# Graph layers on one core: the first range as eight plain products, row sums from sums of quarters, norm steps on ScalarE

## The chip, the core and the metric

One core of one Trainium2 chip runs the whole program. The metric is device time in microseconds (us) of one execution. A ratio in this text is the mean time of one kernel's fast runs over the mean of the fast runs of the kernel before in the same rounds on the same chip, so it is not quite the ratio of the medians that are quoted beside it; its interval is 95%.

Engines: PE is TensorE, PEld its weight loads, DVE is VectorE, ACT is ScalarE, POOL is GpSimd, SP is the engine that issues most loads (SPq its queue). L288 is line 288 of the kernel in question; line numbers differ between kernels.

## The reference, cut to what matters

The program has four layers of a graph network on 2708 nodes with 512 features; `adj` is 2708 x 2708, dense in memory. The change touches layer 0 ("sweep 0" in this text) and, for row sums, layer 1's attention ("sweep 2").

```python
mask = adj > 0                                            # layer 0
head = mask / sqrt(sum(mask, -1))                         # one number per row: a count
inc  = adj + head
x = layernorm(x + (inc @ x) / sum(inc, -1))               # product, row sums, norm
# ... layer 1: e = where(adj != 0, exp(-leaky(scores)), 0)
#              x_a = (e @ h) / (sum(e, 1) + 1e-5)         # row sums again
# ... layers 2 and 3: four more products with adj
```

So a range of output rows can be multiplied only after the rows' nonzero entries have been counted, and divided only after the rows of `inc` have been summed.

## The kernel before

Each product with the adjacency is cut into four *ranges* of 256 to 384 columns (r = 0 to 3). In a range the adjacency (transposed) falls into quarters 11, 12, 21, 22 and X into B11, B12, B21, B22; one level of a Strassen-like scheme replaces eight products of quarters by seven, P1 to P7, at the price of sums on VectorE. A product is 22 f32 matmuls. `at(position, f)` puts work at a position counted in products, and from these positions the order of every engine's queue is fixed when the kernel is built (not by position alone, as the traces below show): at run time each engine works through its own queue and waits: in the changed kernel a preparation of VectorE whose row was ready at 45.3 us began at 50.12, behind seven operations of its queue that waited for their load until 47.55.

```python
FIRST = dict(P1=0, P2=1, P7=2, P5=3, P6=4, P4=5, P3=6)    # order of products in range 0
RING = 44                                                 # one ring of [128, 384] buffers

def count_tile(R0, n, h, i, t=None):      # count the nonzeros of output half h
    if t is None:
        t = trans("cl")                                   # a slot of the same ring
        nc.sync.dma_start(out=t[:w, :n], in_=adjT[...])   # loaded for the count alone
    m = mask_tile()                                       # 3 buffers
    nc.scalar.activation(m[:w, :n], t[:w, :n], AF.Sign)
    nc.scalar.activation(m[:w, :n], m[:w, :n], AF.Relu)
    ...
        nc.tensor.matmul(cnt[h][...], m[...], ones_bf[:w, 0:1], ...)

# extra0, range r: the counts of the NEXT range lie among this range's products
for h, p in ((0, 1.0), (1, 3.8)):
    for i in range(NT):                                   # NT = 22 tiles
        at(pb + p + 2.5 * i / NT, lambda i=i, h=h: count_tile(R1, n1, h, i))
    at(pb + p + 2.55, lambda h=h: count_row(R1, n1, h))

def prep0(r, R0, n, h, hj, k, a):         # adj + head, then the running row sum
    t = trans("s")
    nc.vector.scalar_tensor_tensor(t, a, 0.0, row[R0, h], ALU.is_gt, ALU.mult)
    nc.vector.tensor_tensor(a, a, t, ALU.add)
    add_run(R0, h, n, w, a)                               # 44 additions a range

def layernorm(dsts, y, w):
    ...
    nc.gpsimd.tensor_tensor(rstd[:w, 1:2], rstd[:w, 0:1], neg_half[:w], ALU.pow)
    for d, c0, c1 in dsts:
        nc.vector.tensor_scalar(d[:w], y[:w, c0:c1], mv[:w, 0:1], rstd[:w, 1:2],
                                ALU.subtract, ALU.mult)
```

## Time and profile before

Median 3285.5 us (3284.5 to 3289.4). Columns: stretch, its length, then busy us and instructions of PE, PEld, DVE, ACT, POOL, then granted TensorE clock, DMA share, GB/s. Kernel before, ranges 0 to 3 of sweep 0:

```profile
61.06:151.40 90.34, 83.71 (x480) 68.78 (x480) 64.59 (x197) 43.51 (x98) 4.59 (x6) 0.96 0.55 165
151.40:283.47 132.07, 124.17 (x527) 74.27 (x527) 104.00 (x264) 47.82 (x101) 12.07 (x19) 0.93 0.64 162
283.47:423.01 139.54, 125.67 (x555) 76.24 (x554) 105.22 (x273) 45.62 (x102) 17.76 (x29) 0.95 0.60 132
423.01:533.96 110.95, 103.63 (x442) 73.24 (x441) 95.69 (x275) 6.12 (x12) 28.48 (x51) 0.95 0.68 140
```

| | before |
|---|---|
| first product starts | 61.1 us |
| range 0, then ranges 1 + 2 + 3 | 90.3, then 382.6 us |
| sweep 1 starts, and from there to the end | 534.0, 2754.3 us |

### The profile page before, as it was taken

The numbers are of one execution on the slowest core, as the hardware profiler recorded it, in microseconds if no ns is written. First come the engines' busy times: TensorE is split into PE (matmuls) and PEld (weight loads), VectorE is DVE, ScalarE is ACT, GpSimd is POOL, SyncE is SP. The second block draws the span as 40 slices with busy tenths as digits, with TensorE's granted clock in tenths as the row PEclk, the third lists the DMA queues.
The fourth block names the chain that finished last, engine by engine and source line by source line (L and its number), as shares of the span: only waits on it lengthen the run. The fifth ranks groups of instructions, "written<-read, shape, count | busy, mean of one in ns | idle before, by whom it ended". The sixth has DMA issues, their size and how long they took to land.

```text
span 3288.3 us, 35613 instructions
## 1 busy us (share of the span) xinstructions
PE 3166.4 (96%) x12046; PEld 2050.3 (62%) x12046; DVE 1648.1 (50%) x4093; ACT 567.6 (17%) x1126; POOL 349.1 (11%) x604
## 2 busy tenths in 40 slices
PE   3998999999999999999999999999999999999998
PEld 2755566556765555764556865568656587655675
DVE  6687687334346865975223333323244243643444
ACT  4432500000025544641000000000000000000000
POOL 2001023000000010113000010000011011300000
PEclk9999998999999999999999999999999999999999
DMA  6665665422434342553432453324444344533340
GB/s 201 205 145 121 169 97 138 93 70 50 93 81 111 100 134 80 147 163 118 108 98 72 121 159 90 108 71 116 130 128 125 89 142 130 179 112 99 108 128 33
DMA packets 268683, 383.21 MB, mean 117 GB/s; under 512 B 35199, under 2 KB 230071, under 8 KB 268500
## 3 DMA queue, kind: packets, MB, share of 16 engines
q1 hardware_dynamic: 231096, 291.61, 34.0%
q0 software_dynamic: 28688, 78.49, 7.6%
q10 hardware_dynamic: 8716, 10.84, 1.1%
q8 instruction: 95, 1.56, 0.2%
q14 instruction: 88, 0.72, 0.1%
HBM read 325.31 MB, written 55.49 MB: 116 GB/s over the span
## 4 chain that ended last, share of the span: by engine, by line
PE 83%; issue 6%; DVE 4%; DMA 4%; POOL 2%; ACT 0%; SPq 0%; POOLq 0%; ACTq 0%; DVEq 0%
PE accu L283 21%; PE accc L283 20%; PE accd L283 20%; PE acca L283 10%; PE ps_d L381 8%; DMA cl<-in_adjT 1%; PE ps_n L367 1%; POOL B L177 1%; POOL rstd L343 1%; DMA a<-in_adjT 1%; PE ps_t L373 1%; PE pz L606 1%; DVE T L158 0%; DVE run L444 0%; DVE s L449 0%
## 5 line engine op out<-in xcount | busy, mean ns | idle before, releaser
L250 DVE TENSOR_TENSOR a<-a,a 128x384 f32<-128x384 f32 (+4 forms) x988 | 485.0, 507 | 260.1 <-DMA a<-in_adjT 107.8
L283 PE MATMUL accu<-a,B 128*128 128x384 f32 (+5 forms) x1232 | 395.1, 464 | 0.0
L283 PE MATMUL accc<-s,T 128*128 128x384 f32 (+5 forms) x1232 | 373.3, 458 | 3.6 <-DVE s L250 3.6
L283 PE MATMUL accd<-a,B 128*128 128x384 f32 (+5 forms) x1232 | 376.4, 451 | 0.0
L283 PE MATMUL acca<-a,B 128*128 128x384 f32 (+5 forms) x1232 | 367.7, 452 | 0.0
L283 PE MATMUL accd<-a,T 128*128 128x384 f32 (+5 forms) x1232 | 364.2, 453 | 0.3 <-DVE a L250 0.3
L283 PE MATMUL accu<-a,T 128*128 128x384 f32 (+5 forms) x1232 | 360.6, 450 | 0.0
L283 PE MATMUL accc<-a,T 128*128 128x384 f32 (+5 forms) x1200 | 354.5, 452 | 0.0
L250 DVE TENSOR_TENSOR s<-a,a 128x384 f32<-128x384 f32 (+4 forms) x332 | 166.8, 506 | 318.2 <-PE accc L283 263.7
L283 PEld LDWEIGHTS accc<-s,T 128*128 128x128 f32 (+1 forms) x1232 | 233.8, 194 | 115.8 <-issue 6.7
L283 PEld LDWEIGHTS accd<-a,T 128*128 128x128 f32 (+1 forms) x1232 | 233.3, 191 | 114.6 <-issue 2.4
L283 PEld LDWEIGHTS accu<-a,B 128*128 128x128 f32 (+1 forms) x1232 | 233.0, 196 | 111.5 <-issue 23.8
L283 PEld LDWEIGHTS accu<-a,T 128*128 128x128 f32 (+1 forms) x1232 | 231.7, 190 | 110.5
L283 PEld LDWEIGHTS accc<-a,T 128*128 128x128 f32 (+1 forms) x1200 | 226.1, 190 | 112.6 <-ACT W L304 2.2
L283 PEld LDWEIGHTS accd<-a,B 128*128 128x128 f32 (+1 forms) x1232 | 226.5, 190 | 106.2 <-issue 13.5
L283 PEld LDWEIGHTS acca<-a,B 128*128 128x128 f32 (+1 forms) x1232 | 228.6, 190 | 102.9
L311 DVE TENSOR_TENSOR W<-W,accd 128x384 f32<-128x384 f32 (+2 forms) x56 | 28.1, 505 | 313.9 <-PE accd L283 311.7
L311 DVE TENSOR_TENSOR W<-W,U 128x384 f32<-128x384 f32 (+2 forms) x56 | 28.3, 509 | 280.2 <-ACT U L304 279.2
L444 DVE TENSOR_TENSOR run<-run,a 128x384 f32<-128x384 f32 (+5 forms) x328 | 165.2, 505 | 0.6
L343 POOL TENSOR_TENSOR rstd<-rstd,neg_half 128x1 f32<-128x1 f32 (+1 forms) x88 | 54.8, 623 | 1039.8 <-DVE rstd L342 1034.0
L304 ACT COPY U<-accu 128x384 f32<-128x384 f32 (+2 forms) x56 | 24.4, 439 | 584.9 <-PE accu L283 583.7
L641 ACT ACTIVATE e<-row,neg_s 128x384 f32<-128x384 f32 (+4 forms) x176 | 100.8, 573 | 96.5 <-DVE a L644 32.1
(178 smaller groups left out, 2997.6 us busy)
## 6 DMA issues: line engine op xcount, KB each, us to landing
a<-in_adjT SPq DMA_DIRECT2D x560, 192.0 KB
a<-in_adjT SPq DMA_DIRECT2D x280, 165.0 KB
a<-in_adjT SPq DMA_DIRECT2D x273, 128.0 KB
cl<-in_adjT SPq DMA_DIRECT2D x80, 192.0 KB
ld<-X SPq DMA_DIRECT2D x60, 256.0 KB
Y<-y POOLq DMA_DIRECT2D x54, 256.0 KB, 2.3
B<-Y POOLq DMA_DIRECT2D x84, 128.0 KB, 3.4
X<-o POOLq DMA_DIRECT2D x36, 256.0 KB, 3.2
```

What stands on the lines that cost most here:

```text
L177: eng.dma_start(out=t[:w], in_=q)
L250: nc.vector.tensor_tensor(A[r, dst, k][:w, :n], A[r, a, k][:w, :n], A[r, b, k][:w, :n], op)
L283: nc.tensor.matmul(B[home, c][:, :n], X[STAT[p], k][:w, c * P : (c + 1) * P], A[r, MOV[p], k][:w, :n], start=bool(start and k == k0), stop ...
L304: nc.scalar.copy(T[nm, c][:, :n], B[home, c][:, :n])
L311: nc.vector.tensor_tensor(d[:, :n], T[t, c][:, :n], o[:, :n], ALU.add)
L343: nc.gpsimd.tensor_tensor(rstd[:w, 1:2], rstd[:w, 0:1], neg_half[:w], ALU.pow)
L367: nc.tensor.transpose(ps[:w, c * P : (c + 1) * P], C[h, c][:, lo : lo + w], ident)
L373: nc.tensor.transpose(ps[:, c, :w], cols(dsts, c)[:w], ident[:w, :w])
L381: nc.tensor.matmul(ps[:w], lhs(c), wts[c], start=c == 0, stop=c == DC - 1)
L444: nc.vector.tensor_tensor(run[R0, h][:w, :n], run[R0, h][:w, :n], t[:w, :n], ALU.add)
L606: nc.tensor.matmul(pz[:w], C[h, c][:, lo : lo + w], wab_sb[:, c, :], start=c == 0, stop=c == DC - 1)
L641: nc.scalar.activation(e[:w, :n], row[R0, h][0][:w, :n], AF.Exp, bias=neg_s[:w, t : t + 1])
```

## The change

Its intent: start the first product as soon as quarters 11 and 12 and one count are there, instead of after two counts and the sums of X; take work off VectorE, which TensorE waits for at the borders of ranges. Three parts: (F) range 0 as eight plain products, ordered by output half, its own counts between them, X's sums moved out of its way; (S) row sums from the sums 21+22 and 12+11 that the seven-product scheme makes anyway, half as many additions; (N) the normalising step of sweep 0's norm on ScalarE.

```diff
-FIRST = dict(P1=0, P2=1, P7=2, P5=3, P6=4, P4=5, P3=6)
+FIRST = [("11", "B11", "a"), ("12", "B21", "a"), ("11", "B12", "b"), ("12", "B22", "b"),
+         ("21", "B11", "c"), ("22", "B21", "c"), ("21", "B12", "d"), ("22", "B22", "d")]
@@ loads and preparation of range 0
-                when = {"11": (-4.0, 0.2), "12": (-3.8, 0.2), "21": (-0.3, 0.4), "22": (0.2, 0.4)}
+                when = {"11": (-4.0, 0.2), "12": (-3.8, 0.2), "21": (-2.4, 0.4), "22": (-1.6, 0.4)}
@@ comb: (S)
                 nc.vector.tensor_tensor(A[r, dst, k]..., A[r, a, k]..., A[r, b, k]..., op)
+                if sums and (dst, a) in (("21", "21"), ("12", "12")):
+                    add_run(R0, int(dst == "21"), n, w, A[r, dst, k])
@@ prep0 (in sweep 2's preparation the call goes altogether)
-        add_run(R0, h, n, w, a)
+        if r == 0:
+            add_run(R0, h, n, w, a)
@@ layernorm: (N)
+        if on_scalar:
+            nc.vector.scalar_tensor_tensor(rstd[:w, 0:1], mv[:w, 0:1], -1.0, rstd[:w, 1:2], ALU.mult, ALU.mult)
         for d, c0, c1 in dsts:
+            if on_scalar:
+                nc.scalar.activation(d[:w], y[:w, c0:c1], AF.Identity, bias=rstd[:w, 0:1], scale=rstd[:w, 1:2])
+                continue
@@ extra0: (F) both counts of range 0 read the tiles of the products; half 0's masks on VectorE
+                       lambda h=h, i=i, q=q: count_tile(R0, n, h, i, A[0, q, i % KT], h == 0))
+                at(pb + (-2.0 if h == 0 else 1.4), lambda h=h: count_row(R0, n, h))
@@ X of sweep 0: B11 on ScalarE's queue, B21, B12, B22 on the sync queue; the sums late in range 0
-        at(0.6 + f, lambda k=k: x_sums(k))
-    at(4.0, start0)
+        at(6.0 + 0.9 * f, lambda k=k: x_sums(k))
+    at(2.6, start0)
 # ... cut: the plain products, their copies out, run_sums, positions
```

More of the change, by code (lines that the diff above doesn't have):

```diff
@@ L155, in x_sums @@
         b11, b21, b22 = (X[s, k] for s in ("B11", "B21", "B22"))
-        for d, i, j in (("T3", b22, b), ("T1", b, b11), ("T2", b22, "T1"), ("T4", b21, "T2")):
+        for d, i, j in (("T1", b, b11), ("T2", b22, "T1"), ("T4", b21, "T2"), ("T3", b22, b)):
             j = X[j, k] if isinstance(j, str) else j
-            nc.vector.tensor_tensor(new_x(d, k)[:w], i[:w], j[:w], ALU.subtract)
+            o = b if d == "T3" and ("B12", k) in X else new_x(d, k)
+            nc.vector.tensor_tensor(o[:w], i[:w], j[:w], ALU.subtract)
+        X.pop(("B12", k), None)
     def b12_tile(k):
@@ L215, in sweep, with load @@
     def sweep(base, nk, ranges, prep=None, extra=None, done=None, evac=None, ext_src=None, lead=0.0, first=False,
-              late=None):
+              late=None, sums=False):
         A, spare = {}, {}
         for r, (R0, n) in enumerate(ranges):
-            pb = base + 7 * r
-            ph = FIRST if first and r == 0 else PLAIN
+            plain = first and r == 0
+            pb = base + 7 * r - plain
+            ph = PLAIN
             ks = range(nk)
-            def load(ij, k, R0=R0, n=n, r=r, ph=ph):
+            def load(ij, k, R0=R0, n=n, r=r, plain=plain):
                 hi, hj = int(ij[0]) - 1, int(ij[1]) - 1
                 w = wt(k)
-                if ph is FIRST and ij == "22" and k >= KT - 8:
+                if plain and ij == "22" and k >= KT - 8:
                     i = k - (KT - 8)
@@ L244, in prepare, with comb @@
                 prep(r, R0, n, int(ij[0]) - 1, int(ij[1]) - 1, k, A[r, ij, k])
-            def comb(dst, a, b, op, k, n=n, r=r):
+            def comb(dst, a, b, op, k, n=n, r=r, R0=R0):
                 w = wt(k)
@@ L250, in comb @@
                 nc.vector.tensor_tensor(A[r, dst, k][:w, :n], A[r, a, k][:w, :n], A[r, b, k][:w, :n], op)
+                if sums and (dst, a) in (("21", "21"), ("12", "12")):
+                    add_run(R0, int(dst == "21"), n, w, A[r, dst, k])
             when = {"11": (-1.0, 1.0), "21": (-0.4, 1.0), "22": (0.5, 1.0), "12": (2.4, 1.0)}
             cw = {"s3": 0.3, "s1": 1.1, "s2": 2.1, "s4": 5.05}
-            if ph is FIRST:
-                when = {"11": (-4.0, 0.2), "12": (-3.8, 0.2), "21": (-0.3, 0.4), "22": (0.2, 0.4)}
-                pw = {"11": (-0.9, 1.0), "12": (-0.4, 1.0), "21": (0.6, 1.0), "22": (1.2, 1.0)}
-                cw = {"s3": 1.2, "s1": 2.1, "s2": 3.1, "s4": 5.05}
-            else:
-                pw = {ij: (p + 0.3 - lead * 0.0, f) for ij, (p, f) in when.items()}
+            pw = {ij: (p + 0.3, f) for ij, (p, f) in when.items()}
+            if plain:
+                when = {"11": (-4.0, 0.2), "12": (-3.8, 0.2), "21": (-2.4, 0.4), "22": (-1.6, 0.4)}
+                pw = {"11": (-0.9, 0.6), "12": (-0.3, 0.6), "21": (1.5, 1.5), "22": (3.0, 1.5)}
             for ij in ("11", "21", "22", "12"):
@@ L266, in sweep @@
                         at(pb + p + f * k / nk, lambda ij=ij, k=k, prepare=prepare: prepare(ij, k))
-            for k in ks:
+            for k in ks if not plain else ():
                 f = 0.75 * k / nk
@@ L285, in step, with plain_step @@
                                      skip_group_check=True)
-            for p, i in ph.items():
+            def plain_step(i, k, B=B, n=n, r=r):
+                ij, st, home = FIRST[i]
+                w = wt(k)
+                for c in range(2):
+                    if k == 0 and i % 2 == 0:
+                        B[home, c] = bank("acc" + home)
+                    nc.tensor.matmul(B[home, c][:, :n], X[st, k][:w, c * P : (c + 1) * P], A[r, ij, k][:w, :n],
+                                     start=i % 2 == 0 and k == 0, stop=i % 2 == 1 and k == nk - 1)
+            if plain:
+                for i in range(8):
+                    for k in ks:
+                        at(pb + i + k / nk, lambda i=i, k=k, step=plain_step: step(i, k))
+            for p, i in ph.items() if not plain else ():
                 order = list(ks)
@@ L316, in sweep, with whole @@
             e = 1.02
-            at(pb + ph["P1"] + e + (late or 0 if r == 0 else 0), lambda f=copy_out: f("P1c", "u"))
-            at(pb + ph["P7"] + e, lambda f=copy_out: f("W", "c"))
-            at(pb + ph["P5"] + e, lambda f=add: f("W", "W", "d", None, None))
-            at(pb + ph["P6"] + e, lambda f=copy_out: f("U2", "u"))
-            at(pb + ph["P6"] + e + 0.02, lambda f=add: f("W", "W", "U2", 1, 1))
-            at(pb + ph["P2"] + e, lambda f=add: f("P1c", "P1c", "a", 0, 0))
-            at(pb + ph["P4"] + e, lambda f=add: f("C21", "U2", "c", 1, 0))
-            at(pb + ph["P3"] + e, lambda f=add: f("U2", "U2", "d", 0, 1))
+            if plain:
+                def whole(home, h, e, C=C, B=B, n=n):
+                    for c in range(2):
+                        C[h, 2 * e + c] = tmp("C")
+                        nc.scalar.copy(C[h, 2 * e + c][:, :n], B[home, c][:, :n])
+                for i, (home, h, e) in enumerate((("a", 0, 0), ("b", 0, 1), ("c", 1, 0), ("d", 1, 1))):
+                    at(pb + 2 * i + 2.02, lambda a=(home, h, e), f=whole: f(*a))
+            else:
+                at(pb + ph["P1"] + e + (late or 0 if r == 0 else 0), lambda f=copy_out: f("P1c", "u"))
+                at(pb + ph["P7"] + e, lambda f=copy_out: f("W", "c"))
+                at(pb + ph["P5"] + e, lambda f=add: f("W", "W", "d", None, None))
+                at(pb + ph["P6"] + e, lambda f=copy_out: f("U2", "u"))
+                at(pb + ph["P6"] + e + 0.02, lambda f=add: f("W", "W", "U2", 1, 1))
+                at(pb + ph["P2"] + e, lambda f=add: f("P1c", "P1c", "a", 0, 0))
+                at(pb + ph["P4"] + e, lambda f=add: f("C21", "U2", "c", 1, 0))
+                at(pb + ph["P3"] + e, lambda f=add: f("U2", "U2", "d", 0, 1))
             if extra is not None:
@@ L330, in sweep, with layernorm @@
                 last = r == len(ranges) - 1
-                p0 = pb + (6.08 if h else 7.06)
+                p0 = pb + (6.08 if h else 7.06) if not plain else pb + (8.08 if h else 4.08)
                 done(p0, 0.12 if last and not h else 0.3, last, R0, n, h, C,
                      [(h * KT + k, k * P - R0, wt(k)) for k in ts])
-    def layernorm(dsts, y, w):
+    def layernorm(dsts, y, w, on_scalar=False):
         st = small.tile([P, 6], F32, name="st")
@@ L400, in tiles_of, with count_tile @@
         return list(range(R0 // P, (R0 + n + P - 1) // P))
-    def count_tile(R0, n, h, i, t=None):
+    def count_tile(R0, n, h, i, t=None, on_vector=False):
         w = wt(i % KT)
@@ L409, in count_tile @@
         m = mask_tile()
-        nc.scalar.activation(m[:w, :n], t[:w, :n], AF.Sign)
-        nc.scalar.activation(m[:w, :n], m[:w, :n], AF.Relu)
+        if on_vector:
+            nc.vector.tensor_scalar(m[:w, :n], t[:w, :n], 0.0, None, ALU.is_gt)
+        else:
+            nc.scalar.activation(m[:w, :n], t[:w, :n], AF.Sign)
+            nc.scalar.activation(m[:w, :n], m[:w, :n], AF.Relu)
         if i == 0:
@@ L450, in prep0, with run_sums @@
         nc.vector.tensor_tensor(a[:w, :n], a[:w, :n], t[:w, :n], ALU.add)
-        add_run(R0, h, n, w, a)
-    def run_sums(R0, n, h, after):
+        if r == 0:
+            add_run(R0, h, n, w, a)
+    def run_sums(R0, n, h, after, quarters=True):
         ps = bank("rs", [P, 4])
-        t = run.pop((R0, h))
+        t = run[R0, h] if h and quarters else run.pop((R0, h))
+        if quarters and h == 0:
+            o = run.pop((R0, 1))
+            nc.vector.tensor_tensor(t[:, :n], t[:, :n], o[:, :n], ALU.add)
         ts = list(range(R0 // P, (R0 + n + P - 1) // P))
@@ L466, in extra0 @@
         if r == 0:
-            for i in range(NT):
-                at(pb - 3.7 + 0.05 * i,
-                   lambda i=i: count_tile(R0, n, 0, i, A[0, "11" if i < KT else "12", i % KT]))
-            at(pb - 2.0, lambda: count_row(R0, n, 0))
-            for i in range(NT):
-                at(pb - 1.5 + 0.06 * i, lambda i=i: count_tile(R0, n, 1, i))
-            at(pb - 0.05, lambda: count_row(R0, n, 1))
+            for h in range(2):
+                for i in range(NT):
+                    q = f"{h + 1}{i // KT + 1}"
+                    at(pb + (-3.7 + 0.05 * i if h == 0 else 0.2 + 0.05 * i),
+                       lambda h=h, i=i, q=q: count_tile(R0, n, h, i, A[0, q, i % KT], h == 0))
+                at(pb + (-2.0 if h == 0 else 1.4), lambda h=h: count_row(R0, n, h))
         if r + 1 < len(RANGES0):
@@ L482, in inverse @@
             nc.vector.reciprocal(o, s)
-        for h in range(2):
-            at(pb + 4.5 + 0.05 * h, lambda h=h: run_sums(R0, n, h, inverse))
+        at(pb + (6.0 if r else 2.5), lambda: run_sums(R0, n, 0, inverse, r > 0))
+        at(pb + (2.6 if r else 4.9), lambda: run_sums(R0, n, 1, inverse, r > 0))
     def done0(p0, dp, last, R0, n, h, C, tiles):
@@ L498, in b @@
                 o = targets(t, last and not h, "o")
-                layernorm(o, y, w)
+                layernorm(o, y, w, not last)
                 store(X1[t], o, w)
@@ L542, in start0, with x0_load @@
             nc.vector.tensor_copy(vmat[:, c, 2:4], wab_sb[:, DC + c, :])
+    def x0_load(k, s):
+        if s == "B12":
+            X["B12", k] = b12[k] = X["T3", k] = feat_tile("T3", k)
+            nc.sync.dma_start(out=b12[k][: wt(k)], in_=x_source(X0, k)[1])
+        else:
+            x_load(X0, k, s, nc.scalar if s == "B11" else nc.sync)
     for k in range(KT):
         f = k / KT
-        at(-3.0 + f, lambda k=k: x_load(X0, k, "B11", nc.scalar))
-        at(-0.8 + f, lambda k=k: x_load(X0, k, "B21", nc.gpsimd))
-        at(-0.2 + f, lambda k=k: x_load(X0, k, "B22", nc.gpsimd))
-        at(0.0 + f, lambda k=k: x_load(X0, k, "B12", nc.gpsimd))
-        at(0.6 + f, lambda k=k: x_sums(k))
-    at(4.0, start0)
-    sweep(S[0], KT, RANGES0, prep=prep0, extra=extra0, done=done0, first=True, lead=0.3)
+        at(-5.0 + f, lambda k=k: x0_load(k, "B11"))
+        at(-4.5 + 0.3 * f, lambda k=k: x0_load(k, "B21"))
+        at(-4.0 + 0.3 * f, lambda k=k: x0_load(k, "B12"))
+        at(-3.0 + 0.3 * f, lambda k=k: x0_load(k, "B22"))
+        at(6.0 + 0.9 * f, lambda k=k: x_sums(k))
+    at(2.6, start0)
+    sweep(S[0], KT, RANGES0, prep=prep0, extra=extra0, done=done0, first=True, lead=0.3, sums=True)
     next_x(S[1], X1, True)
@@ L644, in prep2 @@
         nc.vector.scalar_tensor_tensor(a[:w, :n], a[:w, :n], 0.0, e[:w, :n], ALU.not_equal, ALU.mult)
-        add_run(R0, h, n, w, a)
     def extra2(pb, r, R0, n, A):
@@ L659, in extra2 @@
         at(pb - 1.0, lambda: rows(1))
-        for h in range(2):
-            at(pb + 4.5 + 0.05 * h, lambda h=h: run_sums(R0, n, h, share))
+        at(pb + 6.0, lambda: run_sums(R0, n, 0, share))
+        at(pb + 2.6, lambda: run_sums(R0, n, 1, share))
     def done2(p0, dp, last, R0, n, h, C, tiles):
@@ L708, in done2 @@
             at(q + 0.5 + 0.6 * dp * i, f)
-    sweep(S[2], KT, RANGES, prep=prep2, extra=extra2, done=done2, lead=0.3)
+    sweep(S[2], KT, RANGES, prep=prep2, extra=extra2, done=done2, lead=0.3, sums=True)
     def hop_done(dst):
```

## The prediction

> **What bounds the kernel now.** I read the page first (busy shares and the 40 slices), then busy time by stretches cut at the borders of ranges, then the chain of waits at the start, then who waited for whom in each range, and last the order of instructions on TensorE and VectorE. The page and the table of stretches (columns: stretch, length, then busy time and count of PE, PEld, DVE, ACT, POOL, then clock, DMA share, GB/s):
>
> ```profile
> PE 3166.4 (96%) x12046; PEld 2050.3 (62%) x12046; DVE 1648.1 (50%) x4093; ACT 567.6 (17%) x1126; POOL 349.1 (11%) x604
> ...
> 0.00:61.10 61.10, 10.60 (x93) 6.61 (x94) 29.41 (x92) 31.32 (x90) 20.30 (x41) 1.00 0.85 258
> 61.10:143.30 82.20, 79.77 (x455) 65.54 (x455) 58.63 (x181) 42.44 (x96) 2.33 (x3) 0.98 0.52 154
> 143.30:283.40 140.10, 128.00 (x552) 77.47 (x552) 109.85 (x280) 48.89 (x103) 14.32 (x22) 0.93 0.65 168
> 283.40:423.00 139.60, 125.73 (x555) 76.24 (x554) 105.28 (x273) 45.62 (x102) 17.76 (x29) 0.95 0.60 132
> 423.00:534.00 111.00, 103.68 (x442) 73.28 (x441) 95.74 (x275) 6.12 (x12) 28.48 (x51) 0.95 0.68 140
> 534.00:634.00 100.00, 93.27 (x410) 55.87 (x409) 53.80 (x186) 6.26 (x12) 20.84 (x36) 0.91 0.40 84
> ...
> 900.00:1680.00 780.00, 773.86 (x2665) 468.19 (x2664) 483.56 (x1180) 294.30 (x515) 89.83 (x150) 1.00 0.40 114
> ```
>
> TensorE is the bound at 96% busy, so only its 122 us of idle time, its slow-clock time and its own work can change the end. Idle lies in two places. The first 61 us hold no product: 50.5 us idle. The four ranges of sweep 0 that follow lose 2.4 + 12.1 + 13.9 + 7.3 us idle, and the clock there is 0.93 to 0.98. Sweep 2 (inside 900 to 1680) loses at most 6.1 us in 780 at clock 1.00, so work removed from VectorE there is worth next to nothing.
>
> The chain at the start (start, length, what) and TensorE's order there:
>
> ```profile
> 43.71 0.82 ACT mask L410 x2
> ...
> 52.67 5.46 DMA cl<-in_adjT
> 58.21 0.42 ACT mask L410
> 58.66 0.42 ACT mask L411
> 59.13 0.23 PE cnt L416 x2
> ...
> 59.69 0.84 POOL r L431
> 60.58 0.69 PE pr L434 x2
> 61.27 12.12 PE accu L283 x44
> ```
>
> The first product waits for the count of output half 1, which stands before it in TensorE's order. Its 22 tiles "cl" are quarters 21 and 22, loaded for the count alone and loaded again later as "a". The count of half 0 was done long before, and its row was copied out at 28.1 us.
>
> In the ranges TensorE waits for VectorE (here 143.3 to 283.4, then 283.4 to 423; waiter, releaser, total, times, longest):
>
> ```profile
> PE ps_t L373 <- DVE o L345: 7.9, 2, 5.5
> ...
> PE ps_t L373 <- DVE o L345: 6.4, 1, 6.4
> PE accc L283 <- DVE s L250: 3.0, 2, 2.2
> ```
>
> VectorE's order shows why: from 146 to 196 us it runs with no gap over 0.7 us, at one 128x384 operation per 0.47 us (starts of consecutive ones; 0.335 us at 128x256), through preparation, running sums, differences and norms of two ranges at once, while product P1 (14 us) and P7 need its results.
>
> [...] The trace has 550 and 414, and 0.47 and 0.335 from start to start, which is what a stream costs. [...] Here an f32 matmul is recorded as two instructions; 20 of them at 256 columns took 4.32 us (116.89 to 121.21), 0.216 us each[...]. So a product of 22 matmuls takes 44 x 0.216 = 9.5 us at 256 columns, 14.2 at 384 (0.3225 each) and 12.2 at 330. [...] Before, the three issuers together moved 268 to 352 GB/s from 4 to 24 us (291 from 0 to 24); I take 4.16 MB as 14 us at best.
>
> **The change, part by part.**
> *Start.* The first product now needs quarters 11 and 12, the count of half 0 and B11: three times 1354 x 256 x 4 bytes, 4.16 MB. B21, B22 and B12 no longer compete from GpSimd's queue; they stand behind 11 and 12 on one queue. Before, the last tile of 12 was masked at 24.4 us. At 291 GB/s it would land at 14.3; one issuing queue needs 0.33 to 0.43 us an issue and in the trace it often waits for an earlier transfer, so I take 18. Last mask to row was 3.7 us (24.4 to 28.1); the masks are now one VectorE operation instead of two on ScalarE, so 3.5. The first preparation (two operations) adds 0.7. First product: 22.5 us instead of 61.1, 38.6 earlier.
>
> *First range.* Eight products, 76 us. Added to that: [...]2.7 as before (12.16 us for the first 44 instructions against 9.5). The first two products are paced by VectorE: per tile two preparation operations and one running sum, 3 x 0.335 = 1.0 us against 4 x 0.216 = 0.86, so 22.1 for 19, +3.4 with the first latency. Count matmuls now lie inside the stream: 44 of this range and 132 of the next at 0.0725 us (0.22 us for three less the overlap), 12.8. Rows and sums 2.5, waits for GpSimd's power 2. The two tiles of half 0 (1.7 us of transposes and small products each) move into the range, 3.4. Counts of half 1 need quarter 22, the eighth block of 11.1 MB, which lands at 40 to 46 us, while TensorE's fixed order probably has them in the second product, which would end at about 45: I add 4 us. Sum 22.5 + 76 + 2.7 + 3.4 + 12.8 + 2.5 + 2 + 3.4 + 4 = 129.3. Before: 143.3, plus the 3.4 for half 0's tiles that came later, 146.7. Gain 17.4 us, of which the eighth product has already taken 9.5.
>
> *Ranges 1 to 3 of sweep 0.* Their products, counts (9.6; none in the last), seven or six norm tiles at 1.7 and sums make about 123, 121 and 98 us of needed TensorE time, against 140.1, 139.6 and 111: losses 17, 18 and 13. Row sums from sums of quarters remove 22 of 44 additions, and the rest come after VectorE's worst 50 us: 22 x 0.47 = 10.3 us leave that stretch. Taking the normalisation off VectorE leaves a small operation, some 0.4 us less a tile, 1.6. Against it, the first border gets the 44 operations for the sums of X (15 us), of which I expect three quarters earlier, in idle time of the first range, and 3.7 at the border. Net 8 us less at the first border, 12 at the others. I turn that into 7, 10 and 8 us saved, 25 in all.
>
> *The rest.* Sweep 2 also loses 88 additions (about 41 us of VectorE), worth 0 by the table above; the later wait for its row sums may cost 1 or 2 us. The other sweeps are untouched.
>
> Sum: 17.4 + 25 = 42; 3285.5 - 42 = 3243 us.
>
> **Rivals.**
> *The start is bound by loads.* 11.1 MB of X and adjacency now pass mainly on one queue before product 5. Speaking for it: the sync queue issued 22 tiles in 17.7 us, 0.8 us each, and 16 in 13.9 us. At 0.8 us for 77 tiles quarter 22 lands near 60 us, and products 3 to 5 wait: about 15 us of the gain go, 3258. Against it: [...]250 to 276 GB/s still flowed from 40 to 48 us when the sync queue carried nearly all.
> *VectorE ceases to bind sweep 0.* If all the loss in ranges 1 to 3 (48 us) and the 4 us of stall vanish, the gain is 17.4 + 48 + 4 = 69, 3216. For: the waits name VectorE. Against: X sums, transposes waiting through GpSimd and back, and count waits stay.
> *ScalarE's queue takes VectorE's place.* The normalised tile now goes VectorE, GpSimd, VectorE, ScalarE, TensorE; ScalarE also waits for masks. If each of the 18 tiles cost TensorE another 1 us, 18 us are lost, 3261. Against: ScalarE is busy only 35% in these ranges.
>
> **Range and chances.** The start is the firm part, and even that is a net of +38.6 against 21 us put into the stream. The border savings are the soft part, 10 to 48. So 3243, with 3215 to 3266 for 8 in 10. Two per cent is 65.7 us, which needs nearly all the losses of sweep 0 gone: 0.15. Slower by 2% would need a new stall of 100 us: 0.02.
>
> **What would show it.** In the changed profile: first product at 20 to 25 us; 352 product instructions in range 0 and its end at 125 to 134; no "cl" loads before the first product; additions to "run" down by 154; PE's wait for the normalised tile below 10 us over sweep 0 (20.4 from 130 to 500 now); clock 0.97 or more there; from sweep 1 on the same durations within 5 us. It is wrong if the first product starts after 30 us, if a wait on a load or on a count of over 10 us stands between products 1 and 5, if the borders keep their 12 us of idle time, or if sweep 2 changes by over 8 us.

The sum comes to 17.4 + 25 = 42 us, 3243 us. "550 and 414" are the ns that VectorE took for one operation on two tensors at 128x384 and 128x256 in the kernel before. The 2.7 us in the first range are what the first 44 product instructions of the kernel before took beyond 44 x 0.216 us (12.16 against 9.5); why, the trace doesn't show: the granted clock is 1.00 from 61 to 90 us. And 14 us for 4.16 MB is the author's estimate, from the 291 GB/s of the kernel before.

## More of the kernel before

The normalised tile is stored to memory as X1 by GpSimd's queue, and reloaded from there, also by GpSimd's queue, as the X of the next sweep.

What TensorE waited for in ranges 1 and 2 of the kernel before (waiter, releaser, total us, times, longest):

```profile
PE ps_t L373 <- DVE o L345: 11.9, 2, 6.4
PE cnt L416 <- ACT mask L411: 4.2, 2, 2.5
PE accc L283 <- DVE s L250: 3.0, 2, 2.2
```

## The result, and the profile after

The changed kernel took 3306.7 us (median; 3303.5 to 3308.1) against 3285.7 in the same rounds: ratio 1.0061 [1.0043, 1.0078]. It is slower by 21 us where 42 us of gain were predicted (3243 us, with a range of 3215 to 3266). The page of the changed kernel, then the stretches, cut at the first products as above (start, ranges 0 to 3):

```profile
PE 3173.0 (96%) x12090; PEld 2061.7 (62%) x12090; DVE 1577.9 (48%) x3914; ACT 565.3 (17%) x1100; POOL 330.5 (10%) x571
```

```profile
0.00:51.17 51.17, 5.37 (x46) 3.17 (x46) 20.13 (x70) 3.49 (x8) 1.79 (x7) 1.00 0.87 256
51.17:156.99 105.82, 97.52 (x577) 80.03 (x578) 69.51 (x214) 58.14 (x140) 7.04 (x11) 0.95 0.57 149
156.99:291.46 134.47, 122.67 (x520) 73.18 (x519) 86.62 (x217) 54.11 (x107) 10.22 (x15) 0.94 0.57 154
291.46:431.06 139.60, 127.18 (x555) 77.70 (x554) 93.53 (x253) 50.64 (x108) 17.45 (x29) 0.94 0.59 130
431.06:545.34 114.28, 102.80 (x441) 72.93 (x440) 87.45 (x259) 9.38 (x16) 29.46 (x53) 0.94 0.67 139
```

VectorE lost the work that it was to lose: 104.0, 105.2 and 95.7 us busy in ranges 1 to 3 became 86.6, 93.5 and 87.5. The ranges did not get shorter for it: 388.4 us for the three together, against 382.6. TensorE's busy time there is about the same (352.7 and 353.5), its idle time 35.7 us instead of 29.1. The first product starts 10 us earlier, and range 0 takes 15.5 longer. Sweep 1 starts at 545.3 instead of 534.0; from there to the end it is 2756.4 against 2754.3, so the whole story lies in sweep 0. Sweep 2's stretch, 780 us long in both, has 772.3 us of TensorE work after and 773.9 before.

Why the first product starts so late: the chain at the start of the changed kernel (start, length, what).

```profile
20.17 6.67 DMA a<-in_adjT
...
26.96 0.29 DVE mask L443
...
37.82 3.92 DMA T<-in_x
...
43.41 4.04 DMA B<-in_x
...
48.01 2.10 DVE T L161 x6
50.12 0.33 DVE s L484
...
51.17 0.80 PE acca L298
```

The last tile of quarter 12 lands at 26.8 us, and its count is done soon after. But VectorE's queue then has the small products for the attention (vy) and 18 of the first 22 operations of X's sums (T) in it, which wait for B12 and B22 to land, and only behind them the first preparation (s, 50.12) that the first product needs. The sums stand at position 6.0 and this preparation at -1.9, so the order that was built doesn't follow the positions here.

In ranges 1 and 2 TensorE now waits for something else. The changed kernel, same view as before:

```profile
PE cnt L451 <- ACT mask L446: 16.5, 3, 7.0
...
PE ps_t L405 <- ACT o L375: 2.5, 1, 2.5
```

The wait for the normalised tile (11.9 us) and for the sums s (3.0) has gone down to 2.5 and 0.8, as intended. In its place the matmuls of the *next range's count* wait 16.5 us for their masks, against 4.2 before. The longest of them, in the chain of range 2:

```profile
324.27 9.09 DMA cl<-in_adjT
...
333.39 0.49 ACT mask L445
...
333.90 0.49 ACT mask L446
...
334.43 0.28 PE cnt L451 x3
```

A tile "cl", loaded for the count alone, is issued when VectorE has freed a buffer, takes 9.1 us to land, and ScalarE, which waited 10.8 us for it, makes the mask. TensorE waited 7.0 us. That wait costs more than its length. TensorE in steps of 5 us around it, changed kernel (columns: stretch, length, PE busy and instructions, clock, DMA share, GB/s):

```profile
326.00:331.00 5.00, 1.44 (x5) 1.00 0.79 32
331.00:336.00 5.00, 1.57 (x10) 0.51 0.74 162
336.00:341.00 5.00, 5.00 (x17) 0.50 0.27 46
341.00:346.00 5.00, 5.00 (x16) 0.50 0.53 18
346.00:351.00 5.00, 5.00 (x15) 0.79 0.68 152
```

After the gap the clock stands at 0.50 for some 17 us. Summed over steps of 1 us (one minus the clock), the loss at this dip is 8.5 us; at the other five dips that end within sweep 0 it is 3.4, 1.7, 5.1, 3.4 and 5.1 us. From the first product to the start of sweep 1 it is 28.6 us in the changed kernel and 23.9 in the kernel before (21.9 and 19.2 if only time in which TensorE was busy is counted). Over the whole changed kernel it is 46.3 us of 3302, 1.4% (mean granted clock 0.986).

### The profile page after: what moved, and what is told of

Same layout as the page of the kernel before. It is cut to its first block, busy times and chain, and to the rows that moved or that the text cites. A ratio compares the mean times of both kernels' runs of the same rounds, so it can differ in the third digit from the quotient of the medians.

```text
span 3301.7 us, 35430 instructions
## 1 busy us (share of the span) xinstructions
PE 3173.0 (96%) x12090; PEld 2061.7 (62%) x12090; DVE 1577.9 (48%) x3914; ACT 565.3 (17%) x1100; POOL 330.5 (10%) x571
## 4 chain that ended last, share of the span: by engine, by line
PE 82%; issue 6%; DVE 5%; DMA 4%; POOL 2%; ACT 1%; SPq 0%; POOLq 0%; ACTq 0%; DVEq 0%
PE accu L288 21%; PE accd L288 19%; PE accc L288 19%; PE acca L288 10%; PE ps_d L413 8%; PE ps_n L399 1%; DMA cl<-in_adjT 1%; PE acca L298 1%; PE accc L298 1%; PE accb L298 1%; POOL rstd L370 1%; POOL B L181 1%; DVE T L161 1%; PE ps_t L405 1%; DMA X<-o 1%
## 5 line engine op out<-in xcount | busy, mean ns | idle before, releaser
L255 DVE TENSOR_TENSOR a<-a,a 128x384 f32<-128x384 f32 (+4 forms) x963 | 477.3, 509 | 244.1 <-DMA a<-in_adjT 107.1
L288 PE MATMUL accu<-a,B 128*128 128x384 f32 (+5 forms) x1188 | 381.6, 464 | 0.0
L288 PE MATMUL accd<-a,B 128*128 128x384 f32 (+5 forms) x1188 | 365.7, 454 | 0.0
L288 PE MATMUL accc<-s,T 128*128 128x384 f32 (+5 forms) x1188 | 363.8, 461 | 0.9 <-DVE s L255 0.8
L288 PE MATMUL acca<-a,B 128*128 128x384 f32 (+5 forms) x1188 | 354.9, 455 | 0.0
L288 PE MATMUL accd<-a,T 128*128 128x384 f32 (+5 forms) x1188 | 354.2, 457 | 0.0
L288 PE MATMUL accu<-a,T 128*128 128x384 f32 (+5 forms) x1188 | 349.5, 453 | 0.0
L288 PEld LDWEIGHTS accc<-s,T 128*128 128x128 f32 (+1 forms) x1188 | 224.9, 193 | 109.3 <-issue 5.9
L288 PEld LDWEIGHTS accu<-a,B 128*128 128x128 f32 (+1 forms) x1188 | 222.6, 195 | 108.5 <-issue 24.3
L322 ACT COPY U<-accu 128x384 f32<-128x384 f32 (+2 forms) x54 | 23.9, 443 | 597.5 <-PE accu L288 596.3
L407 ACT COPY xT<-ps_t 128x512 f32<-128x512 f32 (+1 forms) x66 | 37.5, 569 | 382.7 <-PE ps_t L405 335.2
```

Source lines behind the costliest of these rows:

```text
L255: nc.vector.tensor_tensor(A[r, dst, k][:w, :n], A[r, a, k][:w, :n], A[r, b, k][:w, :n], op)
L288: nc.tensor.matmul(B[home, c][:, :n], X[STAT[p], k][:w, c * P : (c + 1) * P], A[r, MOV[p], k][:w, :n], start=bool(start and k == k0), stop ...
L407: nc.scalar.copy(t[:, :, :w], ps[:, :, :w])
```

## The experiments

All 18 kernels passed the comparison with the reference. Durations are from the first product of a range to that of the next, from one profile each; the last column is over the kernel before of the same rounds. Runs e1 to e4, e5 to e8, e9 to e12, e13 to e16, and e17 with e18 each shared a chip.

| run | start | range 0 | 1 | 2 | 3 | sweep 1 at | ratio, interval |
|---|---|---|---|---|---|---|---|
| before | 61.1 | 90.3 | 132.1 | 139.5 | 111.0 | 534.0 | 1 |
| after | 51.2 | 105.8 | 134.5 | 139.6 | 114.3 | 545.3 | 1.0061 [1.0043, 1.0078] |
| e1 X sums late | 47.4 | 105.1 | 129.2 | 138.8 | 112.9 | 533.4 | 1.0011 [0.9996, 1.0026] |
| e2 + row on DVE | 33.5 | 114.3 | 131.3 | 139.5 | 117.3 | 535.8 | 1.0003 [0.9986, 1.002] |
| e3 + weights on SP | 27.9 | 114.6 | 128.6 | 138.9 | 114.1 | 524.1 | 0.9979 [0.9964, 0.9994] |
| e4 before + S | 59.6 | 84.9 | 127.3 | 131.6 | 112.2 | 515.6 | 0.9942 [0.9927, 0.9956] |
| e5 before + F | 53.4 | 105.6 | 133.0 | 144.3 | 116.1 | 552.2 | 1.0032 [1.0017, 1.0047] |
| e6 before + N | 61.5 | 88.6 | 135.2 | 141.7 | 113.9 | 540.9 | 1.0006 [0.9991, 1.0021] |
| e7 e4, reloads held | 57.6 | 84.3 | 137.4 | 127.8 | 118.9 | 525.9 | 0.9967 [0.9952, 0.9982] |
| e8 e3 ordered, no N | 30.8 | 109.5 | 125.4 | 138.4 | 116.1 | 520.3 | 0.9937 [0.9921, 0.9954] |
| e9 before + F + S | 53.0 | 106.9 | 138.4 | 135.9 | 116.0 | 550.2 | 1.0033 [1.0021, 1.0045] |
| e10 after, reloads on SP | 53.9 | 106.7 | 137.7 | 137.0 | 118.1 | 553.4 | 1.0055 [1.0043, 1.0067] |
| e11 e4, reloads on SP | 61.3 | 84.9 | 130.0 | 137.4 | 126.3 | 539.9 | 0.9984 [0.9968, 1.0001] |
| e12 e8, masks on DVE | 30.5 | 109.6 | 127.6 | 136.1 | 115.6 | 519.3 | 0.9948 [0.9936, 0.996] |
| e13 after, no cl loads | 52.5 | 94.2 | 116.6 | 128.4 | 116.4 | 508.1 | 0.9912 [0.9895, 0.9928] |
| e14 before, no cl loads | 62.3 | 87.5 | 126.7 | 131.1 | 114.4 | 522.0 | 0.9939 [0.9924, 0.9954] |
| e15 e8, counts later | 30.0 | 103.9 | 116.1 | 130.6 | 116.9 | 497.5 | 0.9875 [0.9861, 0.989] |
| e16 e4, counts later | 61.4 | 95.4 | 117.6 | 128.3 | 117.4 | 520.2 | 0.9943 [0.9928, 0.9957] |
| e17 after, counts later | 51.7 | 95.3 | 116.4 | 128.1 | 111.7 | 503.1 | 0.9916 [0.9894, 0.9938] |
| e18 before, counts later | 61.3 | 104.9 | 128.4 | 135.5 | 112.0 | 542.2 | 1.0025 [1.0008, 1.0041] |

From the start of sweep 1 to the end all of them need 2748 to 2758 us. The start of after, e5, e9, e10, e13 and e17 is the same code and spreads from 51.2 to 53.9 us, so a difference of 3 us in this table means nothing.

### The start: e1, e2, e3

My theory was that the order in the queues, not the loads and not TensorE, holds the first product. Three edits, each on top of the one before.

e1 makes X's sums of sweep 0 all depend on the in-place difference, which can only be made after B12's last use, so they fall behind the first preparations:

```diff
+        if ("B12", k) in X:
+            nc.vector.tensor_tensor(b[:w], b22[:w], b[:w], ALU.subtract)                     # T3, in place
+            nc.vector.tensor_tensor(new_x("T2", k)[:w], b[:w], b11[:w], ALU.add)
+            nc.vector.tensor_tensor(new_x("T1", k)[:w], b22[:w], X["T2", k][:w], ALU.subtract)
+            nc.vector.tensor_tensor(new_x("T4", k)[:w], b21[:w], X["T2", k][:w], ALU.subtract)
```

> Edit: the changed kernel, with the four X sums of sweep 0 written so that all of them hang on the in-place T3, which must wait for the seventh product's use of B12; so VectorE cannot have them ahead of the first preparation. Theory A (the start is held by the fixed order in the engines' queues: VectorE's X sums wait for B12 and B22 ahead of the preparation, and ScalarE's row copy stands behind masks of quarter 21): VectorE is free from 32.5 us, but the row is still copied only at 45.3, so the first product starts at 46 to 47 us (51.2 in the changed kernel) and the time falls by 4 to 6 us. If VectorE's order alone counted, it would start at 33 and the time would fall by 15 to 19. Rival B (loads hold the start, the order only follows them): the start stays at 50 to 52, time within 2 us of the changed kernel. The sums now fall at the border to range 1 (15 us of VectorE there), which may cost range 1 up to 8 us.

First product at 47.4 us: now the row of half 0 came last, copied out by ScalarE, whose queue had masks of quarter 21 ahead of the copy and had waited 43 us for its first tile.

e2 copies that one row on VectorE:

```diff
-        nc.scalar.copy(row[R0, h][:, :n], pr[:, :n])
+        nc.vector.tensor_copy(row[R0, h][:, :n], pr[:, :n])      # range 0, half 0 only
```

> Edit: as e1, and the first row (range 0, half 0) is copied from PSUM by VectorE instead of ScalarE. Theory A: both blocked places are gone; the row is there at 30.5, the weights' products end at 32.5, the first product starts at 33 to 34 us, 17 us earlier than in the changed kernel. How much of that lasts depends on the counts of half 1, whose quarters 21 and 22 land at 42 to 55 us while TensorE's order has those counts inside the first two products: I expect 5 to 10 us to be lost again there, so 7 to 12 us off the changed kernel's time. Rival B (loads): start still above 45, gain below 3 us.

e3 moves the loads of w_sa, a_sa and the two small ones, which ScalarE's empty queue had issued from 10 us on, beside the loads of quarter 12, to the sync queue, where they stand behind all of range 0's tiles:

```diff
-        ws = load_w(w_sa, KT)
+        ws = load_w(w_sa, KT, nc.sync)                           # and wab, bab, a_sa
```

> Edit: as e2, and the weights w_sa, wab, bab and a_sa of the later gate are loaded from the sync queue at their place in the order instead of from ScalarE's idle queue, so that 1.5 MB no longer competes with quarter 12. Theory A with loads as the second limit: the last tile of quarter 12 lands at 19 to 22 us instead of 26.9, first product at 24 to 27 us; quarters 21 and 22 land at about the same time as before or 3 us earlier, so the end of range 0 improves on e2 by only 0 to 5 us. If the start were still a matter of order alone, quarter 12 would land at 26 as before and the start stay at 31 to 33.

First product at 33.5 and 27.9 us. So the three queue positions account for 23 of the 29 us by which the start missed the prediction. What reaches the end is another matter. e1 starts only 4 us before the changed kernel and is 0.5% faster (different rounds), where 4 to 6 us were expected; this stays open. e2 starts 14 us before e1 and reaches sweep 1 2 us after it, with range 0 9 us longer. e3 is 0.8% better than the change (different rounds).

### The parts alone: e4, e5, e6, and F with S: e9

e4 puts only the hunks of the row sums into the kernel before, e6 only those of the norm; e5 is the changed kernel with both undone, e9 with the norm undone.

> Edit: the kernel before, with only the row sums taken from the sums of quarters (all ranges of sweeps 0 and 2). The step of my prediction (VectorE's throughput binds the borders of sweep 0; four borders here): 10 to 25 us faster than the kernel before, with TensorE's idle time in ranges 1 to 3 down from 33 to below 20 us. Rival (the borders are set by waits that do not shorten with VectorE's load: GpSimd's queue, where the power of the norm stands behind reloads of X1 that wait for their store, and the loads for the next counts): within 5 us of the kernel before, idle time in ranges 1 to 3 still 25 us or more though VectorE's busy time falls by 60 us.

> Edit: the changed kernel with the other two parts undone: row sums as before (44 additions a range in sweeps 0 and 2), norm on VectorE. Only the first range differs from the kernel before. If the three parts add up (whole change +16 to +21 us, row sums alone -19), first range and norm together cost 35 to 40, and this run is 25 to 40 us slower than the kernel before, ranges 1 to 3 of sweep 0 together no shorter than the 383 us of the kernel before. Rival (the first range by itself is nearly neutral, and it is the combination that takes the gain of the row sums away): within 12 us of the kernel before. My prediction's step (first range alone gains 17 us) would make it 17 us faster.

> Edit: the kernel before, with only the normalisation of sweep 0 on ScalarE. Theory C: the step is on a chain, not on VectorE's throughput: each tile goes GpSimd, VectorE, ScalarE, and then its store and the reload of X1 that GpSimd's next power stands behind, so every tile gets about 0.5 us later: 2 to 8 us slower, TensorE's wait for the normalised tile not shorter than the 20 us of the kernel before over 130 to 500 us. My prediction's step: 1.6 us off VectorE at each border, so 2 to 5 us faster.

> The changed kernel with the normalisation put back on VectorE: first range and row sums together, without the norm part. Alone, the first range cost +0.32% and the row sums gave -0.58%; their sum is 0.997. Theory 1, the first range and the row sums get in each other's way: 1.003 to 1.006, range 2 of sweep 0 stays at 137 to 140 us. Theory 2, the normalisation on ScalarE, which there stands in one queue with masks that wait for loads, spoils the combination: 0.996 to 0.999, range 2 back at 131 to 133 us. I lean to theory 1, since the run e8, which has no norm part either, had 138.4 us in range 2.

The row sums give 0.58% (e4's 19 us lie in its expected 10 to 25, but TensorE's idle time in ranges 1 to 3 fell only from 29.1 to 25.3 us, not below 20; its mean granted clock is 0.991, against 0.986 to 0.988 in the kernel before), the first range costs 0.32%, the norm does nothing that can be told from zero (+0.06%). Added up that is -0.20%, and the whole change measured +0.61%. e9 (1.0033, where the two parts' sum is 0.9974) shows that F and S get in each other's way without N. TensorE's wait for the next range's count in ranges 1 and 2 tells where: 4.6 us with S alone (e4), 7.8 with F alone (e5), and with both (e9):

```profile
PE cnt L451 <- ACT mask L446: 19.7, 5, 9.3
```

With both, the count also comes sooner in TensorE's order, though its positions are the same. The first count matmul of range 1 stands behind 92 product instructions of that range in the kernel before (44 make a product), 84 in e4, 88 in e5, 68 in e9 and 66 in the changed kernel; in range 2 behind 94, 88, 94, 88 and 82. Whether N costs another 0.3% on top (1.0061 against 1.0033) isn't settled, since the two were not run in the same rounds.

### GpSimd's queue: e7, e10, e11

The next theory was that the normalised tile comes late because GpSimd's power stands in its queue behind reloads of X1 that wait for X1's store to land: in the changed kernel VectorE waited 26.1 us for GpSimd in sweep 0 after range 0, 9.4 at the longest. e7 holds a quarter of the reloads back by giving them the buffer of T3, e10 and e11 issue all of them from the sync queue:

```diff
-    next_x(S[1], X1, True)
+    next_x(S[1], X1, True, q=nc.sync)      # e10; e11 the same on e4
```

> Edit: e4 (row sums only), and the reloads of B12 of X1 for sweep 1 go into the slot of T3, which comes free only after the last use of T3 in sweep 0, so that GpSimd does not meet them in ranges 2 and 3. Theory D (what is left at the borders is GpSimd's queue: the power of the norm stands behind reloads that wait 7 to 8 us for their store to land): TensorE's wait for the normalised tile falls from 13 us in e4 (2.0, 2.7 and 8.6 in ranges 1, 2, 3) to below 6; range 2 gains up to 3 us, range 3 gains little unless the reloads of B11 there go too; 2 to 8 us faster than e4. Rival (VectorE's load is still what is left): no change, within 2 us of e4.

> The changed kernel with the reloads of X1 for sweep 1 issued from the sync queue instead of GpSimd's, so that GpSimd's power no longer stands behind a reload that waits for its store to land. GpSimd theory: GpSimd's waits on DMA X<-o vanish from ranges 2 and 3 (20 to 24 us now), VectorE's wait for GpSimd falls below 3 us at the longest (9.43 now), ranges 2 and 3 take 245 us together instead of 253.9: ratio 1.002 to 1.004. Rival, VectorE's own pace: the waits go but the two ranges stay within 3 us of 253.9: 1.005 to 1.007. Second rival, the wait only changes queue: the sync queue stands still for 7 to 14 us behind a reload and a load of adjacency comes late, 1.006 or more, with PE or VectorE waiting on DMA a.

> Before plus the row sums (e4, 0.9942; ranges 2 and 3 of sweep 0 take 131.6 and 112.2 us there), with the reloads of X1 for sweep 1 on the sync queue. GpSimd theory: ranges 2 and 3 lose another 6 to 10 us together, ratio 0.991 to 0.993. Rival, pace or moved wait: 0.994 to 0.996.

In e10 from 298 to 553 us, the waits of VectorE and of the sync queue:

```profile
DVE rstd L371 <- POOL rstd L369: 4.3, 9, 0.7
```

```profile
SPq L181 <- DMA X<-o: 69.0, 7, 21.1
```

VectorE's wait for GpSimd has shrunk, from 26.1 us to 6.8 over ranges 1 to 3 and to 0.7 at the longest, and ranges 2 and 3 take 255.1 us instead of 253.9, so the theory of GpSimd as the cause of the loss fell. Which rival was right isn't settled: the time (1.0055) and the two ranges lie where the first rival put them, while the wait of the second is there, on the sync queue, where everything behind the reload stands still for up to 21.1 us. e11 (0.9984) is worse than e4 (0.9942) and than both of its forecasts. e7 missed too: it is 8 us slower than e4 (different rounds), with range 1 longer by 10 us, range 2 shorter by 4 and range 3 longer by 7.

### The order in range 0: e8, e12

e8 takes e3, loads quarters 21 and 22 before B12 and B22, B21 on ScalarE's queue, and has the norm on VectorE. e12 makes the masks of range 0's second count on VectorE.

```diff
-        at(-4.0 + 0.3 * f, lambda k=k: x0_load(k, "B12"))
-        at(-3.0 + 0.3 * f, lambda k=k: x0_load(k, "B22"))
+        at(-2.3 + 0.3 * f, lambda k=k: x0_load(k, "B12"))
+        at(-1.9 + 0.3 * f, lambda k=k: x0_load(k, "B22"))
-                       lambda ...: count_tile(R0, n, h, i, A[0, q, i % KT], h == 0))    # e12 only
+                       lambda ...: count_tile(R0, n, h, i, A[0, q, i % KT], True))
```

> Edit: the first range mended further: e3, with B21 loaded from ScalarE's queue after B11, quarters 21 and 22 loaded before B12 and B22, and the norm on VectorE as in the kernel before. Theory A: the first product starts at 25 to 28 us, the wait for the counts of half 1 (9.8 us in e3) falls below 4, range 0 takes 104 to 110 us and ends at 130 to 136; ranges 1 to 3 as in e4 (127, 132, 112) but for up to 5 us more in range 1 for the X sums: 3255 to 3265 us on e4's scale (3271), the best so far. If ranges 1 to 3 take as long as in e3 (128.6, 138.9, 114.1), the norm on ScalarE was not what lengthened them, and the time is 3268 to 3275.

> e8 (0.9937; range 0 takes 109.5 us, TensorE waits 9.3 us there for count masks of ScalarE) with the masks of the second count of range 0 on VectorE as well. Theory, ScalarE's queue held the count: that wait falls below 3 us, range 0 takes 100 to 104 us, ratio 0.991 to 0.993. Rival, VectorE is full in products 1 and 2: 22 masks of 0.335 us more (7.4 us) come back as TensorE's wait on prepared tiles, range 0 stays at 107 to 110, ratio 0.993 to 0.995.

e8 is 0.9937. Its wait for counts in range 0 is 9.3 us, not below 4, and ranges 2 and 3 (138.4 and 116.1 us) are no shorter than in e3, so the norm on ScalarE was not what lengthened them. e12 left range 0 where it was; TensorE's waits in its range 0:

```profile
PE cnt L456 <- DVE mask L448: 5.2, 3, 4.2
PE cnt L456 <- ACT mask L451: 2.7, 3, 1.5
```

The wait for ScalarE fell from 9.3 to 2.7 us, as expected, and a wait for the same masks on VectorE took its place: the rival came nearer.

### The loads of the counts: e13, e14

What was left was the count of the next range. e13 and e14 keep all its masks and matmuls but read one tile of ones that stays in place, so that its 22 loads for each half and their ring slots go. The counts are then wrong.

```diff
-            t = trans("cl")
-            j0 = (i // KT) * NH + (i % KT) * P
-            nc.sync.dma_start(out=t[:w, :n], in_=adjT[j0 : j0 + w, h * NH + R0 : h * NH + R0 + n])
+            t = still                      # e14: for ranges 1 to 3 only
+    still = ring_tile("still")
+    nc.gpsimd.memset(still, 1.0)
```

> The changed kernel, where the counts of the next range take their masks from one tile of ones that stays in place instead of tiles loaded for the count (a wrong result on purpose: every count is the number of rows). All masks and count matmuls stay; only the loads and their ring slots go, less one slot that the tile of ones keeps. Theory, the count's loads and slots hold TensorE: its wait for count masks (16.5 us in ranges 1 and 2) vanishes and with it the half-clock stretches after it (about 8 us of lost speed), ranges 1 and 2 take 250 to 260 us together instead of 274.1, ratio 0.998 to 1.001. Rival, VectorE's pace and the way of the normalised tile over GpSimd: 268 to 275 us, 1.004 to 1.006.

> The control: the kernel before with the same tile of ones for the counts of ranges 1 to 3 (wrong result on purpose). It had no wait for count masks over 1 us in ranges 1 and 2 (271.6 us together). If the count's loads are the difference between the two kernels, this gains little: 264 to 271 us, ratio 0.997 to 1.000. If it gains as much as e13 does, the loads burden both kernels alike and are not the cause of the difference.

A slip in the second text: it says that the kernel before had no such wait over 1 us in ranges 1 and 2; it had the 4.2 us shown above. e13 is 0.9912, better than I gave the theory: 1.5% under the changed kernel (0.9912 / 1.0061), while e14 gains 0.6%. TensorE's wait for count masks in ranges 1 and 2 is nil in both, and the clock loss of sweep 0 falls to 10.2 us in e13. Ranges 1 and 2 fall from 274.1 to 245.0 us after, and from 271.6 to 257.8 before. So these loads burden both kernels, and the changed one by 29 us more (0.9%). Of that, 17 us lie in ranges 1 to 3 (e13 saves 27.0 us there, e14 10.4) and 9 in range 0, which holds the counts of range 1. e13 takes away the loads, their ring slots and their place in the sync queue at once, and doesn't tell the three apart.

### The counts later: e15, e16, e17, e18

These keep the loads and move the counts to a place where products have freed ring slots:

```diff
-            for h, p in ((0, 1.0), (1, 3.8)):
+            for h, p in ((0, 2.2), (1, 4.2)):
-                    at(pb + p + 2.5 * i / NT, lambda i=i, h=h: count_tile(R1, n1, h, i))
-                at(pb + p + 2.55, lambda h=h: count_row(R1, n1, h))
+                    at(pb + p + 1.8 * i / NT, lambda i=i, h=h: count_tile(R1, n1, h, i))
+                at(pb + p + 1.85, lambda h=h: count_row(R1, n1, h))
```

> e8 (0.9937; ranges 1 and 2 take 263.8 us, wait for count masks 5.8 us) with the next range's counts later, half 0 from 2.2 to 4.0 products into the range instead of 1.0 to 3.5, half 1 from 4.2 to 6.0 instead of 3.8 to 6.3, when products 2 to 4 have freed ring slots. Theory: that wait falls below 2 us and ranges 1 and 2 take 255 to 260 us, ratio 0.991 to 0.993. Rival: the rows come too late for the preparation of the next range, and the wait moves to VectorE's tiles: 263 to 270 us, 0.994 to 0.996.

> e4 (before plus row sums, 0.9942; ranges 1 and 2 take 258.9 us, wait for count masks 4.6 us) with the counts moved in the same way. Theory: 253 to 257 us, ratio 0.992 to 0.994. Rival, rows too late: 259 to 266 us, 0.995 to 0.997.

> The changed kernel with the counts moved later as in e15 and nothing else altered (the late start and the norm on ScalarE stay). Theory, the place of the counts is what the borders lost: the wait for count masks in ranges 1 and 2 falls from 16.5 us to below 3, those ranges take 248 to 256 us together instead of 274.1, ratio 0.997 to 1.000. Rival, e15's gain needed its other mends: 262 to 274 us, ratio 1.002 to 1.006.

> The control: the kernel before with the counts moved later. Range 0 should lose about 10 us as in e16 (95.4 against 84.9), because with seven products and 22 tiles loaded for its own count it has less room; ranges 1 and 2 should gain 5 to 12 us of 271.6. Ratio 0.998 to 1.003. If it gains over 0.5%, the place of the counts is worth the same in both kernels and is no cause of the difference.

e17, the changed kernel with these three lines and nothing else, is 0.9916 (3260.9 us against 3288.6): faster than its expectation, 1.4% under the change itself (0.9916 / 1.0061, different rounds). The same stretches as above, and TensorE's wait for count masks in ranges 1 and 2, both of e17:

```profile
51.71:146.96 95.25, 93.52 (x577) 76.57 (x577) 68.48 (x212) 56.78 (x140) 7.94 (x11) 1.00 0.64 161
146.96:263.33 116.37, 114.88 (x519) 69.57 (x518) 87.41 (x221) 49.75 (x107) 10.47 (x16) 1.00 0.65 181
263.33:391.46 128.13, 123.64 (x555) 75.19 (x554) 93.58 (x254) 47.94 (x108) 16.58 (x29) 0.97 0.63 144
391.46:503.13 111.67, 101.98 (x441) 72.41 (x440) 86.66 (x254) 9.37 (x16) 29.78 (x54) 0.95 0.63 139
```

```profile
PE cnt L451 <- ACT mask L446: 1.6, 3, 0.7
```

e15, e16 and e17 all did better in ranges 1 and 2 than expected (246.7, 245.9 and 244.5 us). e17 has the same instructions as the changed kernel; TensorE is idle for 1.7, 1.5 and 4.5 us in ranges 0 to 2 and the clock is 1.00 in the first two. From its first product to the start of sweep 1 the clock costs it 9.2 us, against 28.6; of the 43 us by which that stretch is shorter, 15 are loss while TensorE was busy (21.9 us in the changed kernel, 6.6 in e17). In the trace the first count matmul of range 2 stands 43.0 us into the range in the changed kernel, 47.8 in the kernel before and 56.2 in e17. The sync queue shows the ring's part: before loads "cl" in ranges 1 and 2 it waited 24.5 us for products with accc, which free a slot, in the changed kernel (16.7 in the kernel before); in e17 this wait is gone.

The control e18 lost 0.25%: range 0 became 15 us longer and ranges 1 and 2 only 8 us shorter. e16 is where e4 was: it gained 13 us in ranges 1 and 2 and lost 16 in ranges 0 and 3. So the place of the counts is worth 1.4% in the changed kernel and less than nothing in the kernel before. That its range 0 has one product less and loads 22 tiles for a count of its own is a likely reason, not a tested one. e15, which adds the earlier start and has the norm on VectorE, is the best kernel that was run: 3255.8 us against 3296.1, 1.25% faster than before and about 1.9% faster than the change (0.9875 / 1.0061, different rounds). No run tried a larger ring instead.

## Why the prediction was wrong, point by point

The predicted start of sweep 1 was 42 us earlier than before; in the profile it is 11.4 later. The 53 us between them are 29 at the start and 31 at the borders, less 1 that range 0 was shorter than predicted, and less 5 because the prediction ended the old range 0 at 146.7, where the first product of range 1 began at 151.4.

**TensorE is the bound, sweep 2 is worth nothing.** Right. VectorE lost 28 us of work in sweep 2's stretch (about 41 were expected) and TensorE's busy time there did not move by more than 2 us. Additions to `run` fell by 154, as written (336 to 182).

**The start, "First product: 22.5 us instead of 61.1".** Wrong: 51.2. The step added up what the first product *needs* (11, 12, a count, a row, one preparation), and took it for granted that each engine turns to it when its inputs are there. Queue order was the missing term: VectorE had the sums of X in front, ScalarE the masks of quarter 21, and the loads of w_sa went out beside those of quarter 12 (moved behind them in e3: from 33.5 to 27.9 us). e1 to e3 measured the three together at 23.3 us; with them out of the way the start is 27.9, 5 us from the estimate. The trace of the changed kernel shows the queue: the preparation whose row was ready at 45.3 us began at 50.12 behind seven T operations that waited for B22 until 47.55. I did not ask in which order the change would put the two. The rival "the start is bound by loads" was right in a part: quarter 12 landed at 26.8 us instead of 18, and the last load of quarter 22, which I had landed at 40 to 46, was issued only at 53.5. With so late a start little waited for it.

**Range 0, from 22.5 to 129.3, so 106.8 us of length.** The size was right, 105.8, but by luck, since its make-up was not. e17 does the same work in 95.3 us with 93.5 busy at a granted clock of 1.00. The other 10 us are waits for count masks (5.7 us, none in e17) and for the power (2.4, against 1.6), and a clock of 0.50 after them (5.1 us lost, part of it in idle time), where I had put more TensorE time for counts and tiles.

**The borders, "I turn that into 7, 10 and 8 us saved, 25 in all".** Wrong: 5.8 us lost. The mechanism was right as far as it went: VectorE was relieved, and the wait for the normalised tile and for s fell from 14.9 to 3.3 us in ranges 1 and 2. But the step treated VectorE as the only thing waited for. In the combination of F and S the next thing in line held TensorE: the count of the next range, whose tiles share one ring and one queue with the adjacency, 16.5 us of waiting where there had been 4.2, and a clock of 0.50 around each of the three waits (5.1, 3.4 and 8.5 us lost). A faster VectorE alone did not bring it about (4.6 us in e4); with F and S together the count also came sooner in TensorE's order. The prediction said of a rival that "count waits stay", named a wait on a count as a sign only for range 0, and had ScalarE's masks in its last rival, but not the loads that stand behind them. The runs that settle it: e13 (loads away, counts kept, 17 us more in ranges 1 to 3 than in the control) and e17 (counts moved, ranges 1 to 3 take 356.2 us; 382.6 - 25 is 357.6). That e17 meets the predicted sum is partly luck: the same move shortens these ranges of the kernel before to 375.9 (e18), so against its control the change is worth 19.7 of the 25 us.

**"ScalarE's queue takes VectorE's place".** Partly. The normalised tile from ScalarE made TensorE wait 8.1 us at the longest, in range 3; alone (e6) the part is 1.0006. Its real cost in the combination stays open.

**"VectorE ceases to bind sweep 0".** This rival, 69 us of gain, did not come about. e17 (3260.9 against 3288.6) and e15 reach 28 and 40 us, both with the counts moved.

What stays open: why the built order places the counts sooner when F and S are together, though their positions are the same; and e15's range 0 (103.9 us) is 9 us longer than e17's, so an early start is in part still given back inside range 0.

## What to carry to other kernels

When work is taken off the engine that others wait for, ask which wait is second in line, price the gain only down to that one, and ask whether the change itself moves it; here a queue of loads with a shared ring of buffers was next, and three changed lines of positions turned a loss of 0.6% into a gain of 0.8%. To predict a start, list for each engine what stands in its queue ahead of the needed instruction, not only what the instruction needs. Here waits of TensorE cost more than their length: a clock of 0.50 came with each of the three count waits of 4.0 to 7.0 us (17.1 us lost), and in e17 with a single wait of 2.4 us (3.4 lost). And count matmuls of 0.28 us for three, placed among the products in TensorE's order, held the products behind them for 16.5 us in ranges 1 and 2.
